# Four-bank score tiles and denominators summed on GpSimd in a graph attention layer

## The chip, the cores and the metric

The kernel runs on one core of a Trainium2 chip. The metric is the device time of one execution in microseconds, lower is better. A core has five engines that run their own instruction queues in order and wait for each other through semaphores: TensorE (PE in the profile, with its weight loads as PEld), VectorE (DVE), ScalarE (ACT), GpSimd (POOL) and SyncE (SP). Matrix products land in PSUM, which has eight banks of 512 fp32 values on each of 128 partitions.

## The reference

Four graph layers are applied to 16 graphs of 1024 nodes with 128 features, each with its own 1024x1024 adjacency of zeros and ones. Each layer normalises the features, takes a relu, computes its own aggregation and adds the result to `x`. The change lies in the second layer, a four-head softmax attention whose scores are offset by the logarithm of the adjacency:

```
def _L1_gnn_ref(x, edge_weight, Wq, bq, Wk, bk, Wv, bv, Wo, bo):
    NH = 4; HD = HID // NH; SCALE = HD ** (-0.5); EPS = 1e-08
    ...
    scores = jnp.einsum('chqd,chkd->chqk', q, k) * SCALE
    scores = scores + jnp.log(jnp.maximum(edge_weight, EPS))[:, None, :, :]
    attn = jax.nn.softmax(scores, axis=-1)
    out = jnp.einsum('chqk,chkd->chqd', attn, v)
    ...
    return out @ Wo.T + bo
```

The third layer (a graph attention without query-key products, `gat` below) and the fourth (a normalised graph convolution, `gcn` below) use the same adjacency and run next to the attention.

## The kernel before

The kernel has three stages, one after another: a dilation of the adjacency, the first layer, and a stage with the other three layers (`attentions_plain`). Only the last one is touched. It starts near 2960 us of the profiled span and lasts to the end.

**Jobs side by side.** The stage loops over the batch `b` from -1 to 16. In each turn `side_by_side` interleaves up to four generators, one step of each at a time by weights: `attend` for graph b (weight 21), `gat` then `gcn` for graph b-1 (45), and `matrix` and `before`, which load the adjacency and make queries, keys and values for graph b+1 (9 each). The order in which the generators emit instructions is only a start: the tile framework then places the instructions in each engine's queue, and puts a semaphore wait on every use of a buffer whose last user is on another engine. A tile of a pool with `bufs=n` can be written again when the use of the n-th tile before it has ended.

**The attention of one graph.** `attend` goes over two halves of 512 query nodes (`hf`), and in each over eight blocks of 128 key nodes (`k`). For one k:

- L1214: four matmuls, one for each head, of 32 rows by 128 columns, give the scores of 128 keys by 512 queries into four PSUM tiles of one bank each (pool `f_ps`, four buffers). They use four different row groups of the array.
- L1217: four matmuls of the adjacency block with 16 times the identity add the logarithm term to each tile.
- L1219: four ACT instructions take the exponential, one bank each, into SBUF tiles `e`.
- L1206 (`weigh`, for the block k-1): four matmuls with the values (`va`) add to one bank `acc`, each head in its own 32 partitions, and four with a matrix of ones (`ones_hd`) add the denominators to a second bank, `den`.

After the eight blocks L1227 takes the reciprocal of the denominators on DVE and L1228 multiplies. An fp32 matmul shows as two records in the trace, so eight records of L1214 are the four heads.

**What runs beside it.** In `gat`, GpSimd multiplies the values by exponentials (L1259, L1261), ACT and DVE split them into three bf16 parts (L677 to L680, a helper), L1289 multiplies A by the parts, and for each head DVE makes a masked matrix `pm` from `dst`, `minus` and A in eight instructions (L1273, function `positive`), which 128 matmuls of L1302 use; DVE reduces each pair of their results (L1304). Two PSUM buffers `sum` serve all of these. L1310 to L1320 close the layer. Each layer's `normal` (L1128 to L1149) is a chain of DVE statistics, a power on GpSimd (L1142) and eight ACT instructions (L1148). `gcn` uses L1326, the splitter, L1338, L1343 and L1350. `matrix` checks each adjacency block on DVE (L1111) and takes a power on GpSimd (L1126). `before` adds a bias on GpSimd (L1178).

Of the kernel before, what the change touches and what calls it, by code (L numbers as in the profile page):

```python
# [7 lines left out]
F32 = mybir.dt.float32  # L8
# [4 lines left out]
AF = mybir.ActivationFunctionType  # L13
ALU = mybir.AluOpType
AX = mybir.AxisListType
PSUM = bass.MemoryType.PSUM
# [3 lines left out]
P = 128  # L20
NB = N // P
H, HD = 4, 32
HN = N // 2
# [986 lines left out]
SIGMA = LOG_EPS / 16.0  # L1010
# [4 lines left out]
def attentions_plain(tc, x1, adj, deg, trouble, eye, Wq, bq, Wk, bk, Wv, bv, Wo, bo, W2, a2, W3, b3, out, bound, reach):  # L1015
    nc = tc.nc
    with ExitStack() as ctx:
        cp = ctx.enter_context(tc.tile_pool(name="f_const", bufs=1))
        small = ctx.enter_context(tc.tile_pool(name="f_small", bufs=4))
        pss = ctx.enter_context(tc.tile_pool(name="f_ps", bufs=4, space=PSUM))  # L1020
        psa = ctx.enter_context(tc.tile_pool(name="f_acc", bufs=2, space=PSUM))
        psg = ctx.enter_context(tc.tile_pool(name="f_sum", bufs=2, space=PSUM))
        xp = ctx.enter_context(tc.tile_pool(name="f_x", bufs=3))
        adp = ctx.enter_context(tc.tile_pool(name="f_adj", bufs=3))
        lp = ctx.enter_context(tc.tile_pool(name="f_load", bufs=2))
        ep = ctx.enter_context(tc.tile_pool(name="f_exp", bufs=8))
        pmp = ctx.enter_context(tc.tile_pool(name="f_pos", bufs=2))
        w2 = ctx.enter_context(tc.tile_pool(name="f_work2", bufs=2))
        w1 = ctx.enter_context(tc.tile_pool(name="f_work1", bufs=1))
# [8 lines left out]
        ident_log = cp.tile([P, P], BF16, name="ident_log")  # L1038
# [3 lines left out]
        ones = cp.tile([P, HD], F32, name="ones_hd")  # L1042
        nc.vector.memset(ones, 1.0)

        def bank(pool=psg, name="sum"):
            return pool.tile([P, HN], F32, name=name)
# [31 lines left out]
        ps = bank()  # L1078
# [13 lines left out]
        ps = bank()  # L1092
# [67 lines left out]
        def natural_times(xT, w, done):  # L1160

            for hf in range(2):
                ps = bank()
                for c in range(4):
                    k = 4 * hf + c
                    nc.tensor.matmul(ps[:, c * P:(c + 1) * P], xT[:, k * P:(k + 1) * P], w, start=True, stop=True)  # L1166
                done(slice(4 * hf, 4 * hf + 4), blocked(ps))
                yield
# [27 lines left out]
        def attend(A, xt, qT, kT, va):  # L1196
            oT = w1.tile([P, N], F32, name="oT")
            for hf in range(2):
                cols = slice(hf * HN, (hf + 1) * HN)
                acc, den = [bank(psa, "acc") for _ in range(2)]  # L1200

                def weigh(k, es):
                    for ps, one in ((acc, False), (den, True)):
                        for hd in range(H):
                            r = slice(hd * HD, (hd + 1) * HD)
                            nc.tensor.matmul(ps[r], ones if one else va[:, k, r], es[hd],  # L1206
                                             start=k == 0, stop=k == NB - 1)

                last = None
                for k in range(NB):  # L1210
                    s = [bank(pss, "t") for _ in range(H)]
                    for hd in range(H):
                        r = slice(hd * HD, (hd + 1) * HD)
                        nc.tensor.matmul(s[hd], kT[r, k * P:(k + 1) * P], qT[r, cols], start=True, stop=False)  # L1214
                    es = []
                    for hd in range(H):
                        nc.tensor.matmul(s[hd], ident_log, A[:, k, cols], start=False, stop=True)  # L1217
                        e = ep.tile([P, HN], F32, name="e")
                        nc.scalar.activation(e, s[hd], AF.Exp, scale=SIGMA)  # L1219
                        es.append(e)  # L1220
                    if last is not None:
                        weigh(k - 1, last)
                    last = es
                    yield
                weigh(NB - 1, last)
                rden = w1.tile([P, HN], F32, name="rden")
                nc.vector.reciprocal(rden, den)  # L1227
                nc.vector.tensor_tensor(oT[:, cols], acc, rden, op=ALU.mult)  # L1228
                yield
            yield from natural_times(oT, wo, lambda c, ps: nc.vector.tensor_tensor(  # L1230
                xt[:, c, :], xt[:, c, :], ps, op=ALU.add))
# [122 lines left out]
        A, ready = {}, {}  # L1354
        for b in range(-1, B + 1):
            jobs = []
            if 0 <= b < B:
                jobs.append((21, attend(A[b], *ready[b])))
            if b >= 1:
                xt = ready[b - 1][0]  # L1360
                jobs.append((45, chain(gat(b - 1, xt, A[b - 1]), gcn(b - 1, xt, A[b - 1]))))
            if b + 1 < B:
                jobs.append((9, matrix(b + 1, A)))
                jobs.append((9, before(b + 1, ready)))
            side_by_side(jobs)
# [49 lines left out]
def whole(tc, x, adj, nodemask, chunk_mats, chunk_mask, eye, sel, p, out):  # L1415
    nc = tc.nc
    with tc.tile_pool(name="dram", bufs=1, space=DRAM) as dp, tc.tile_pool(name="keep", bufs=1) as kp:
        removed = dp.tile([NB, P, P, P], F16, name="removed")
        dilated = dp.tile([B, 2, P, NB, HN], F32, name="dilated")
        x1 = dp.tile([B, N, D], F32, name="x1")  # L1420
        kept = dp.tile([B, P, NB, N], F8, name="kept")
        unsettled = kp.tile([P, 2, NB], F32, name="unsettled")
        trouble = kp.tile([P, B, NB, 3], F32, name="trouble")
        deg = kp.tile([P, B, NB], F32, name="degree")
        bound = kp.tile([P, B], F32, name="bound")
        reach = kp.tile([P, B], F32, name="reach")
        word = kp.tile([1, 1], I32, name="word")
        g = lambda *names: [p["L0_gnn_" + n] for n in names]
        layer0 = [g("Wr1", "Wr2", "Wr3"), g("Wx1", "Wx2", "Wx3"), g("b1", "b2", "b3"), g("g1", "g2", "g3"),
                  g("be1", "be2", "be3"), *g("Wl", "bl")]  # L1430
        weights = [p["L1_gnn_" + n] for n in ("Wq", "bq", "Wk", "bk", "Wv", "bv", "Wo", "bo")]
        weights += [p["L2_gnn_W"], p["L2_gnn_a"], p["L3_gnn_W"], p["L3_gnn_b"]]
        dilate_plain(tc, adj, eye, kept, unsettled)
        convolutions_plain(tc, x, eye, kept, x1, *layer0)
        attentions_plain(tc, x1, adj, deg, trouble, eye, *weights, out, bound, reach)
        verdict(tc, nodemask, unsettled, trouble, deg, bound, reach, word)
        with tc.If(nc.values_load(word[0:1, 0:1], min_val=0, max_val=6 * P) > 0):
            dilate(tc, adj, nodemask, chunk_mats, chunk_mask, removed)
            convolutions(tc, x, adj, nodemask, eye, removed, dilated, x1, *layer0)
            attentions(tc, x1, adj, eye, sel, *weights, out)  # L1440
# [40 lines left out]
```

## Time and profile before

| | |
|---|---|
| median of 3 runs | 5915.55 us (5912.04 to 5918.76) |
| profiled execution, its time | 5929.54 us |
| profiled execution, its span | 5927.7 us |
| PE busy | 4577.2 us, 77% |
| DVE busy | 2813.5 us, 47% |
| ACT busy | 1999.0 us, 34% |
| POOL busy | 1086.7 us, 18% |
| in 2940 to 5760 us: PE, DVE, ACT, POOL busy | 2455.90, 1555.66, 1166.30, 345.81 us |
| granted TensorE clock in 2940 to 5760 us | 0.93 |

The steady turns of the stage (graphs 1 to 15) can be told apart by the first L1289 of each. Two of these starts, 4010.88 and 4194.56 us, are 183.7 us apart, and over all fifteen turns the mean is 180.9 us. In the profile, busy time counts an engine's instructions, a line "idle before" names what ended the wait, and the granted clock is the share of full TensorE speed that was allowed. A POOL or DVE instruction that is held up after it has started shows as a longer instruction, not as a wait.

### The profile page before, as it was taken

The numbers are of one execution on the slowest core, as the hardware profiler recorded it, in microseconds if no ns is written. First come the engines' busy times: TensorE is split into PE (matmuls) and PEld (weight loads), VectorE is DVE, ScalarE is ACT, GpSimd is POOL, SyncE is SP. The second block draws the span as 40 slices with busy tenths as digits, with TensorE's granted clock in tenths as the row PEclk, the third lists the DMA queues.
The fourth block names the chain that finished last, engine by engine and source line by source line (L and its number), as shares of the span: only waits on it lengthen the run. The fifth ranks groups of instructions, "written<-read, shape, count | busy, mean of one in ns | idle before, by whom it ended". The sixth has DMA issues, their size and how long they took to land. (4 is left out here: it accounts for less than half of the span.)

```text
span 5927.7 us, 71034 instructions
## 1 busy us (share of the span) xinstructions
PE 4577.2 (77%) x29914; PEld 2489.5 (42%) x29914; DVE 2813.5 (47%) x4098; ACT 1999.0 (34%) x3265; POOL 1086.7 (18%) x719
## 2 busy tenths in 40 slices
PE   5777775666658886776498888888888888888884
PEld 3444442434344454444334344344343343434443
DVE  4555443222253234323445565555655555555455
ACT  3444443122122221222264344443344434344321
POOL 5611111111140005103511011110111101111001
PEclk8898987777779987998799999999899999999997
DMA  8600004111002211220511011110011100110000
GB/s 277 179 1 1 1 4 161 44 36 43 29 22 71 79 64 43 75 75 15 154 60 33 4 36 36 36 36 11 26 36 36 36 22 15 36 36 29 4 2 8
DMA packets 260322, 283.41 MB, mean 48 GB/s; under 512 B 10508, under 2 KB 225176, under 8 KB 251800
## 3 DMA queue, kind: packets, MB, share of 16 engines
q1 hardware_dynamic: 110232, 203.27, 10.1%
q10 hardware_dynamic: 149760, 75.51, 4.4%
q8 instruction: 236, 3.87, 0.3%
q14 instruction: 94, 0.77, 0.0%
HBM read 228.40 MB, written 50.33 MB: 47 GB/s over the span
## 5 line engine op out<-in xcount | busy, mean ns | idle before, releaser
L1214 PE MATMUL t<-qT,kT 32*128 32x512 f32 x2048 | 550.7, 700 | 205.7 <-ACT e L1219 205.4
L963 PE MATMUL t<-C,parts 128*128 128x512 fp8e4 x2304 | 593.4, 416 | 129.6 <-DVE parts L680 88.3
L1219 ACT ACTIVATE e<-t 128x512 f32<-128x512 f32 x1024 | 530.6, 601 | 471.3 <-PE t L1217 471.1
L1273 DVE SCALAR_TENSOR_TENSOR pm<-dst,minus,A 128x1024 fp8e4<-128x1024 f32 x512 | 646.9, 1334 | 89.8 <-ACT dst L1270 89.8
L1302 PE MATMUL sum<-parts,pm 128*128 128x198 bf16 x4096 | 400.2, 254 | 103.3 <-DVE pos L1304 103.3
L1302 PEld LDWEIGHTS <-pm 128*128 128x128 fp8e4 x4096 | 357.0, 99 | 260.2 <-issue 254.1
L963 PEld LDWEIGHTS <-parts 128*128 128x128 bf16 x2304 | 237.8, 105 | 449.9 <-DVE parts L680 110.6
L968 DVE TENSOR_TENSOR o<-t,rdeg 128x1024 f32<-128x1024 f32 x48 | 58.7, 1224 | 667.4 <-PE t L238 667.4
L1214 PEld LDWEIGHTS t<-qT,kT 32*128 32x128 f32 x2048 | 189.3, 198 | 360.6 <-ACT e L1219 263.2
L219 POOL TENSOR_TENSOR nrm<-nrm,minus_half 128x8 f32<-128x8 f32 x48 | 104.1, 2169 | 1272.7 <-DVE nrm L976 1272.7
L1206 PE MATMUL acc<-e,va 128*32 128x512 f32 x2048 | 329.8, 659 | 0.0
L1206 PE MATMUL acc<-e,ones_hd 128*32 128x512 f32 x2048 | 327.9, 625 | 0.0
L846 PE MATMUL big<-tri,rows 128*128 128x256 fp8e4 (+3 forms) x1344 | 319.3, 375 | 0.0
L1217 PE MATMUL t<-A,ident_log 128*128 128x512 fp8e4 x1024 | 299.8, 415 | 0.0
L1311 POOL TENSOR_TENSOR pos<-pos,ex 128x1056 f32<-128x1056 f32 x16 | 49.0, 3063 | 1306.5 <-DVE pos L1304 1306.5
L225 PE MATMUL t<-ident,h 128*128 128x128 f32 x512 | 88.4, 322 | 252.9 <-ACT h L255 147.1
L851 DVE SCALAR_TENSOR_TENSOR rows<-y,hh,rows 128x1024 fp8e4<-128x1024 f16 x128 | 185.4, 1448 | 196.5 <-ACT y L849 195.3
L1227 DVE RECIPROCAL rden<-acc 128x512 f32<-128x512 f32 x32 | 107.4, 3358 | 355.1 <-PE acc L1206 355.1
L1304 DVE TENSOR_REDUCE pos<-sum 128x132 f32<-128x396 f32 x256 | 141.0, 566 | 271.0 <-PE sum L1302 271.0
L861 ACT CAST rows<-big 128x1024 fp8e4<-128x1024 f32 x128 | 129.5, 1012 | 376.7 <-PE big L860 304.9
L965 ACT COPY aggT<-t 128x1024 f32<-128x1024 f32 x48 | 48.6, 1012 | 562.0 <-PE t L963 562.0
L1270 ACT COPY dst<-sum 128x512 f32<-128x512 f32 x128 | 75.1, 588 | 458.3 <-PE sum L1269 458.3
(256 smaller groups left out, 7989.9 us busy)
## 6 DMA issues: line engine op xcount, KB each, us to landing
a<-in_adj_dram SPq DMA_DIRECT2D x128, 512.0 KB, 3.8
C<-kept SPq DMA_DIRECT2D x48, 1024.0 KB, 4.7
x<-xt ACTq DMA_DIRECT2D x48, 512.0 KB, 2.9
kept<-rows SPq DMA_DIRECT2D x16, 1024.0 KB, 3.8
xt<-in_x_dram ACTq DMA_DIRECT2D x32, 512.0 KB, 3.8
xt<-x ACTq DMA_DIRECT2D x32, 512.0 KB, 3.8
a_row<-in_adj_dram SPq DMA_DIRECT2D x16, 512.0 KB, 6.1
x<-x ACTq DMA_DIRECT2D x16, 512.0 KB, 4.0
```

The lines of the kernel that those rows point to most:

```text
L846: nc.tensor.matmul(ps[:, a:lo + HN], lhs, triF[:, a - t * P:lo + HN - t * P], start=t == 0, stop=t == NB - 1 or t == 3 and lo == 0)
L851: nc.vector.scalar_tensor_tensor(row, y16, hh[:, g:g + 1], row, op0=ALU.not_equal, op1=ALU.mult, saturate=False)
L861: nc.scalar.copy(m[:, g, :, s * P:(s + 1) * P], tr, saturate=False)
L963: nc.tensor.matmul(ps[:, cols], parts[:, k, j, :], C[:, j, cols], start=j == 0 and k == 0, stop=j == NB - 1 and k == 2)
L1206: nc.tensor.matmul(ps[r], ones if one else va[:, k, r], es[hd], start=k == 0, stop=k == NB - 1)
L1214: nc.tensor.matmul(s[hd], kT[r, k * P:(k + 1) * P], qT[r, cols], start=True, stop=False)
L1217: nc.tensor.matmul(s[hd], ident_log, A[:, k, cols], start=False, stop=True)
L1219: nc.scalar.activation(e, s[hd], AF.Exp, scale=SIGMA)
L1227: nc.vector.reciprocal(rden, den)
L1273: nc.vector.scalar_tensor_tensor(pm[:, i, :], dst, minus[:, i, hd:hd + 1], A[:, i, :], op0=ALU.is_ge, op1=ALU.mult, saturate=False)
L1302: nc.tensor.matmul(ps[:, jj * 6 * W:(jj + 1) * 6 * W], pm[:, i, (j + jj) * P:(j + jj + 1) * P], flat(parts4[:, i, hd]), start=i == 0, stop ...
L1304: nc.vector.reduce_sum(pos[:, j:j + 2, hd, :], ps[:, :12 * W].rearrange("p (j s w) -> p j w s", j=2, s=3), axis=AX.X)
```

## The change

The four score tiles of one bank each become one tile of four banks, allocated from a pool with one buffer. The four exponential tiles become one tile of 128x2048 (three buffers), and ACT takes two heads, 1024 elements, in one instruction: 512 instructions in place of 1024. The ones matmuls inside the loop go; instead GpSimd adds each block's exponentials into `total` (128x2048 fp32, seven adds for each half of a graph, 224 in all), and after the last block four matmuls of ones with `total` give the denominators. `weigh(NB - 1)` is followed by one more `yield`.

```
-        pss = ctx.enter_context(tc.tile_pool(name="f_ps", bufs=4, space=PSUM))
+        pss = ctx.enter_context(tc.tile_pool(name="f_ps", bufs=1, space=PSUM))
...
-        ep = ctx.enter_context(tc.tile_pool(name="f_exp", bufs=8))
+        ep = ctx.enter_context(tc.tile_pool(name="f_exp", bufs=3))
...
                 acc, den = [bank(psa, "acc") for _ in range(2)]
 
-                def weigh(k, es):
-                    for ps, one in ((acc, False), (den, True)):
-                        for hd in range(H):
-                            r = slice(hd * HD, (hd + 1) * HD)
-                            nc.tensor.matmul(ps[r], ones if one else va[:, k, r], es[hd],
-                                             start=k == 0, stop=k == NB - 1)
+                total = w1.tile([P, H, HN], F32, name="total")
+
+                def weigh(k, es, before):
+                    for hd in range(H):
+                        r = slice(hd * HD, (hd + 1) * HD)
+                        nc.tensor.matmul(acc[r], va[:, k, r], es[:, hd], start=k == 0, stop=k == NB - 1)
+                    if k:
+                        nc.gpsimd.tensor_tensor(total, before if k == 1 else total, es, op=ALU.add)
 
                 last = None
                 for k in range(NB):
-                    s = [bank(pss, "t") for _ in range(H)]
+
+                    s = pss.tile([P, H, HN], F32, name="t")
                     for hd in range(H):
                         r = slice(hd * HD, (hd + 1) * HD)
-                        nc.tensor.matmul(s[hd], kT[r, k * P:(k + 1) * P], qT[r, cols], start=True, stop=False)
-                    es = []
+                        nc.tensor.matmul(s[:, hd], kT[r, k * P:(k + 1) * P], qT[r, cols], start=True, stop=False)
+                    es = ep.tile([P, H, HN], F32, name="e")
                     for hd in range(H):
-                        nc.tensor.matmul(s[hd], ident_log, A[:, k, cols], start=False, stop=True)
-                        e = ep.tile([P, HN], F32, name="e")
-                        nc.scalar.activation(e, s[hd], AF.Exp, scale=SIGMA)
-                        es.append(e)
+                        nc.tensor.matmul(s[:, hd], ident_log, A[:, k, cols], start=False, stop=True)
+                        if hd % 2:
+                            nc.scalar.activation(es[:, hd - 1:hd + 1], s[:, hd - 1:hd + 1], AF.Exp, scale=SIGMA)
                     if last is not None:
-                        weigh(k - 1, last)
+                        weigh(k - 1, last, first)
                     last = es
+                    first = es if k == 0 else first
                     yield
-                weigh(NB - 1, last)
+                weigh(NB - 1, last, first)
+                yield
+                for hd in range(H):
+                    nc.tensor.matmul(den[hd * HD:(hd + 1) * HD], ones, total[:, hd], start=True, stop=True)
                 rden = w1.tile([P, HN], F32, name="rden")
                 nc.vector.reciprocal(rden, den)
                 nc.vector.tensor_tensor(oT[:, cols], acc, rden, op=ALU.mult)
```

## The prediction

> **What bounds the kernel now.** I read the page's groups first, then the waits of the last stage, then the timeline of one steady turn of the batch loop. The page says what the attention costs PE and what stands beside it on ACT and DVE:
>
> ```profile
> span 5927.7 us, 71034 instructions
> ...
> L1214 PE MATMUL t<-qT,kT 32*128 32x512 f32 x2048 | 550.7, 700 | 205.7 <-ACT e L1219 205.4
> L1219 ACT ACTIVATE e<-t 128x512 f32<-128x512 f32 x1024 | 530.6, 601 | 471.3 <-PE t L1217 471.1
> L1273 DVE SCALAR_TENSOR_TENSOR pm<-dst,minus,A 128x1024 fp8e4<-128x1024 f32 x512 | 646.9, 1334 | 89.8 <-ACT dst L1270 89.8
> ```
>
> PE is the busiest engine (2455.90 of 2820 us between 2940 and 5760), so at first sight its work sets the time. The view of PE's waits in the stage shows the rest, each line with its total, count and longest:
>
> ```profile
> PE t L1214 <- ACT e L1219: 205.4, 61, 6.9
> PE sum L1302 <- DVE pos L1304: 103.3, 34, 8.1
> PE sum L1289 <- DVE parts L680: 46.8, 14, 18.8
> ```
>
> So two places have no slack: where PE waits for DVE, anything that slows DVE is paid at once. The timeline shows them in a turn:
>
> ```profile
> 4179.97 2.82 POOL L1178 TENSOR_TENSOR x<-x,bor 128x1024 f32<-128x1024 f32 x1 [3.76 <-issue]
> 4180.51 11.74 DVE L1273 SCALAR_TENSOR_TENSOR pm<-dst,minus,A 128x1024 fp8e4<-128x1024 f32 x8
> 4192.17 2.34 DVE L680 TENSOR_TENSOR parts<-vals,parts 128x2112 bf16<-128x2112 f32 x1
> ...
> 4194.56 11.44 PE L1289 MATMUL sum<-parts,A 128*128 128x396 bf16 x64 [1.86 <-DVE parts L680]
> ```
>
> Eight pm instructions, then parts, then PE may begin L1289. For each later head it is the same:
>
> ```profile
> 4022.16 1.95 PE L1269 MATMUL sum<-hT,wdst 128*128 128x512 f32 x4
> 4024.76 9.66 DVE L1273 SCALAR_TENSOR_TENSOR pm<-dst,minus,A 128x1024 fp8e4<-128x1024 f32 x8 [1.84 <-ACT dst L1270]
> 4034.34 1.04 DVE L1304 TENSOR_REDUCE pos<-sum 128x132 f32<-128x396 f32 x2
> 4034.95 0.22 PE L1118 MATMUL sum<-A,ident 128*128 128x128 fp8e4 x1 [2.28 <-DVE pos L1304]
> ```
>
> The third thing to see is what a GpSimd instruction does to such a DVE instruction:
>
> ```profile
> 4110.51 2.34 POOL L1326 TENSOR_TENSOR x<-x,b3r 128x1024 f32<-128x1024 f32 x1 [5.62 <-ACT h L1148]
> 4110.97 3.03 DVE L678 TENSOR_TENSOR h<-h,gparts 128x512 f32<-128x512 f32 x2 [5.68 <-ACT gparts L677]
> ...
> L1312 DVE TENSOR_TENSOR tot<-tot,ex 128x1056 f32<-128x1056 f32 x16 | 46.9, 2930 | 0.6
> L1314 DVE TENSOR_TENSOR tot<-tot,pos 128x1056 f32<-128x1056 f32 x16 | 20.1, 1258 | 1.7
> ```
>
> L1312 and L1314 have one shape, but L1312 runs while POOL runs L1311 and takes 1.67 us longer. A lone L678 takes 0.69 us; here the first ends only after POOL has ended at 4112.85. L1273 goes from a minimum of 1270 to a maximum of 3374 ns (the view of its line), and the group at 4180.51 is 2.1 us longer than that at 4024.76, with L1178 beside it. DVE instructions with two SBUF inputs and GpSimd's tensor_tensor take turns, whole instruction by whole instruction; L1178, at 2.82 against 2.34, shows that GpSimd waits its turn too.
>
> **What the Trainium skill says.** "GPSIMD Engine Reference", Specifications, says that GpSimd shares SBUF interfaces with VectorE, with contention for instructions that have two SBUF inputs; the lines above agree and give the size. Its section with measured numbers gives 4497 ns for an fp32 add of 2048 elements. "TensorE: Matmul & The Clock Gate", Part 3, says that column tiles run concurrently and a pack lasts about one matmul; Part 1 there says that an idle window of about 3.4 us halves the clock. The trace agrees with both: 16 records of L1206 occupy 1.86 us, one matmul alone (two records, 4031.62) still 1.05, and after a 5.99 us wait L1214 takes 3.52 in place of 1.14. "PSUM — Partial Sum Buffer", PSUM bank collisions, asks for separation by bank only; the waits of the four-bank tile below therefore come from tracking the tile, not from a need.
>
> **The change part by part.** I counted the instruction order of the two built kernels.
>
> PE work: eight matmuls of `weigh` as one run cost 1.86, so without other effects 256 x 0.93 = 238 go and 32 x 0.97 = 31 come back: -207. But the order no longer keeps them together. Before, the L1206 runs need 556 rounds of up to four; after, the values need 390 (204 are pairs) and the denominators 60. At 0.93 and 0.97 that is 517 against 436: -81. Score runs fall from 393 to 375, -19 at 1.06. Identity matmuls stand mostly in pairs, about 0.53 each against 0.95 for four: +24. The net is -76 us, 5 a turn.
>
> Waits: in the new order the third identity matmul of a block waits for the first exponential of the same block, and the first score matmul for the second one of the block before. An exponential of 1024 I take at 1.03 (a 128x1024 ACT copy from PSUM, L965, is 1012 ns; bounds 0.98 to 1.2). With 0.19 from PE to ACT and 0.04 back, it costs 1.26; a pair of value matmuls hides 0.97. Where the side jobs put L1302 or L1338 there, nothing is seen. Going through one turn I find five gaps of 0.3, one of 1.26 and some of 0.1: 3.3 us a turn. ACT gets less work, and that is worth nothing, since its delays are those of DVE and POOL results ahead in its queue.
>
> GpSimd: an add of 2048 costs from 3.9 (twice L1259's 1.96) to 5.9 (L1311's 3.06 for 1056, scaled). I take 4.6, twice the L1326 row's 2.34 less a fixed part; 14 a turn are 64 us on an engine with some 20 us of work. The sum fits, the turns with DVE do not. I walked the new order through a turn, with the durations above, from its first identity matmul (before: 4151.29, or 3967.6 one turn earlier):
>
> L1289: pm(0) starts on DVE at +29, as before (4180.51). The adds for k=2 and k=3 become ready at 29.6 and 35.5, both inside pm(0), and take 9.2; L1178 now runs ahead, which gives back 2.1. The next add stands behind L1126, which waits for DVE. So 29 + 9.7 + 9.2 + 2.3 = 50 against 43.3: +7. PE would have been ready at 38.
>
> pm(1): the add for k=4 ends 1.4 into it, that for k=5 falls inside it (4.6). +6 and some 2 of extra PE blocks: the next L1269 stands at 87 against 72, +15.
>
> pm(2): the add for k=6 overlaps 1.5, that for k=7 4.6; the denominator matmuls wait for this last add, 2.5 us, inside the same delay. Next L1269 113.6 against 92.4: +21.
>
> pm(3): no add falls in it, since the first block of a half has none.
>
> End of gat: add k=10 gets between L1312 and L1314, +5, and the normalisation behind it holds ACT and so the next exponentials. With PE blocks done meanwhile, L1338 starts at 173 against 155: +18. The tail, three blocks with `gcn` and the second denominators in place of one, adds 6. A turn is 24 us longer; the PE saving and the round trips are in it.
>
> Clock: the waits of 12 and 10 us at L1289 and pm(1), and 13 at the normalisation, make about three more cold starts; each costs some 2 us (3.52 less 1.14). I take 5 a turn, bounds 0 and 8.
>
> Turn 0 has no gat; its blocks take 5 us now and about as much with adds of 4.6; +5 for two exposed last adds.
>
> 15 x (24 + 5) + 5 = 440 on 5929.54 gives 6370 for an execution like the profiled one. The median of runs lies 14 us lower, so 6355.
>
> **The rivals.** First, the collisions are mostly hidden: waits on PE move but DVE catches up. Then -76 + 16 x 3.3 + 16 x 2.5 leaves +17: 5930, up to 6080 with some collisions. The 47% of DVE busy time speaks for it, the zero slack at L680 and pos against it.
>
> Second, faster: the PE saving decides, since PE is the busiest engine. With the -76 alone 5840; with all fours concurrent, 5710. It decides if the adds cost the path less than one add (5 us) a turn. Against it stand the two adds inside pm(0).
>
> Third, heavier: nearly every add lands on the path, or lasts 5.5 and more. 14 x 4.6 less 5 is 59 a turn, 6800.
>
> That the four-bank tile doesn't give four banks of look-ahead is already in the forecast: pairs wait for each other.
>
> **How the numbers follow.** Forecast 0.63, hidden 0.16, faster 0.07, heavier 0.14. Its own bounds (add 3.9 to 5.9, clock 0 to 8, three or seven colliding adds) give 6150 to 6550; reaching a little to both sides, 6110 to 6590. A measurement of this kernel can't tell less than about 0.2% from none. Faster 0.08, same 0.02, slower 0.90.
>
> **What would show it.** Right: L1279 (the pm line after the change) with a mean of 1.7 us or more, POOL L1209 near 4.6 us, PE's wait for parts grown from 46.8 to 150 us or more and that for pos from 103 to 200 or more, and a turn of about 210 us between first L1295s (the new number of L1289). Value pairs at about 0.97 each show the lost saving. Wrong: pm unchanged beside adds, or a turn under 185 us.

## The result and the profile after

The changed kernel takes 6412.28 us (median of 4 runs, 6403.48 to 6419.01). The kernel before took 5917.16 us beside it (4 runs, 5912.04 to 5948.53), so the ratio is 1.0824, with a 95% interval of 1.0784 to 1.0864. The profiled span grew from 5927.7 to 6417.3 us, by 489.6.

The page of the changed kernel has these lines, in the columns known from before:

```profile
span 6417.3 us, 66960 instructions
...
L1209 POOL TENSOR_TENSOR total<-total,e 128x2048 f32<-128x2048 f32 x192 | 898.2, 4678 | 818.4 <-ACT e L1222 817.8
L1279 DVE SCALAR_TENSOR_TENSOR pm<-dst,minus,A 128x1024 fp8e4<-128x1024 f32 x512 | 906.1, 1838 | 90.6 <-ACT dst L1276 90.6
L1222 ACT ACTIVATE e<-t 128x1024 f32<-128x1024 f32 x512 | 522.8, 1021 | 1141.0 <-PE t L1220 1136.9
...
L1209 POOL TENSOR_TENSOR total<-e 128x2048 f32<-128x2048 f32 x32 | 146.0, 4561 | 540.1 <-ACT e L1222 538.5
```

L1279 is the old L1273, unchanged in the code. Its instruction grew from 1334 to 1838 ns, 512 times. PE's waits over the span are:

```profile
PE t L1220 <- ACT e L1222: 325.5, 110, 13.8
PE sum L1295 <- DVE parts L680: 187.5, 16, 18.4
PE sum L1118 <- DVE pos L1310: 116.8, 14, 8.3
PE sum L1308 <- DVE pos L1310: 110.3, 34, 8.3
```

The wait for parts was 46.8. That for pos, at the matmuls of `positive` and at L1118, the identity matmul behind them, was 103.3 and 32.8, 136.1 in all; it is now 110.3 and 116.8, 227.1 in all, so the growth stands at L1118. Its line before was:

```profile
PE sum L1118 <- DVE pos L1304: 32.8, 14, 3.1
```

The timeline of a steady turn shows the first of these waits arise:

```profile
4187.85 18.16 DVE L1279 SCALAR_TENSOR_TENSOR pm<-dst,minus,A 128x1024 fp8e4<-128x1024 f32 x8
4188.62 4.87 POOL L1209 TENSOR_TENSOR total<-total,e 128x2048 f32<-128x2048 f32 x1 [2.91 <-ACT e L1222]
4195.16 4.98 POOL L1209 TENSOR_TENSOR total<-total,e 128x2048 f32<-128x2048 f32 x1 [1.67 <-ACT e L1222]
4205.94 2.35 DVE L680 TENSOR_TENSOR parts<-vals,parts 128x2112 bf16<-128x2112 f32 x1
4208.33 5.12 PE L1295 MATMUL sum<-parts,A 128*128 128x396 bf16 x16 [10.60 <-DVE parts L680]
```

The eight pm instructions took 11.74 us before. Two additions of 4.87 and 4.98 fall inside them, and the eight take 18.16. PE stands for 10.60 us. The second head meets the same:

```profile
4220.73 4.51 POOL L1209 TENSOR_TENSOR total<-total,e 128x2048 f32<-128x2048 f32 x1 [9.73 <-ACT e L1222]
...
4224.79 14.14 DVE L1279 SCALAR_TENSOR_TENSOR pm<-dst,minus,A 128x1024 fp8e4<-128x1024 f32 x8 [1.84 <-ACT dst L1276]
4230.07 5.38 POOL L1209 TENSOR_TENSOR total<-total,e 128x2048 f32<-128x2048 f32 x1 [4.83 <-ACT e L1222]
4239.46 0.26 PE L1118 MATMUL sum<-A,ident 128*128 128x128 fp8e4 x1 [8.34 <-DVE pos L1310]
```

Where the 489.6 us lie is read from the first L1295 of each turn (L1289 before) and the first score matmul of the stage:

| part of the span | before | after | difference |
|---|---|---|---|
| up to the first score matmul | 2961.7 | 2970.7 | 9.0 |
| from there to the first L1295 (turn 0) | 134.6 | 179.1 | 44.5 |
| fifteen turns, mean of one | 180.86 | 209.86 | 15 x 29.0 = 435.0 |
| last first-L1295 to the end | 118.4 | 119.7 | 1.3 |

The first row cannot be put down to the change: over all kernels below, which differ only in code behind it, that start scatters between 2954.1 and 2978.6 us.

### The profile page after: what moved, and what is told of

Same layout as the page of the kernel before. It is cut to its first block, busy times and chain, and to the rows that moved or that the text cites. A ratio compares the mean times of both kernels' runs of the same rounds, so it can differ in the third digit from the quotient of the medians.

```text
span 6417.3 us, 66960 instructions
## 1 busy us (share of the span) xinstructions
PE 4612.0 (72%) x28122; PEld 2425.8 (38%) x28122; DVE 3170.0 (49%) x4098; ACT 1986.5 (31%) x2753; POOL 2117.9 (33%) x943
## 4 chain that ended last, share of the span: by engine, by line
PE 46%; DVE 30%; ACT 9%; POOL 8%; issue 4%; DMA 3%; SPq 0%; ACTq 0%; POOLq 0%; DVEq 0%
DVE pm L1279 14%; PE t L963 8%; PE sum L1308 4%; PE t L238 4%; PE big L846 3%; PE sum L1295 3%; PE sum L1344 3%; PE acc L1207 3%; DVE rows L851 3%; PE t L1217 2%; PE t L1220 2%; PE stat L981 2%; DVE h L678 2%; PE stat L991 1%; DVE h L930 1%
## 5 line engine op out<-in xcount | busy, mean ns | idle before, releaser
L1209 POOL TENSOR_TENSOR total<-total,e 128x2048 f32<-128x2048 f32 x192 | 898.2, 4678 | 818.4 <-ACT e L1222 817.8
L1279 DVE SCALAR_TENSOR_TENSOR pm<-dst,minus,A 128x1024 fp8e4<-128x1024 f32 x512 | 906.1, 1838 | 90.6 <-ACT dst L1276 90.6
L1222 ACT ACTIVATE e<-t 128x1024 f32<-128x1024 f32 x512 | 522.8, 1021 | 1141.0 <-PE t L1220 1136.9
L963 PE MATMUL t<-C,parts 128*128 128x512 fp8e4 x2304 | 592.6, 416 | 130.8 <-DVE parts L680 89.7
L1308 PE MATMUL sum<-parts,pm 128*128 128x198 bf16 x4096 | 433.3, 265 | 110.3 <-DVE pos L1310 110.3
L1207 PE MATMUL acc<-e,va 128*32 128x512 f32 x2048 | 490.3, 688 | 0.3
L1217 PE MATMUL t<-qT,kT 32*128 32x512 f32 x2048 | 474.4, 717 | 12.5 <-ACT e L1222 7.5
L1111 DVE SCALAR_TENSOR_TENSOR junk<-a 128x1024 fp8e4<-128x1024 f32 x128 | 177.7, 1388 | 415.4 <-DMA a<-in_adj_dram 414.8
L1295 PE MATMUL sum<-parts,A 128*128 128x396 bf16 x1024 | 221.9, 380 | 187.5 <-DVE parts L680 187.5
L1209 POOL TENSOR_TENSOR total<-e 128x2048 f32<-128x2048 f32 x32 | 146.0, 4561 | 540.1 <-ACT e L1222 538.5
L1220 PEld LDWEIGHTS <-ident_log 128*128 128x128 bf16 x1024 | 82.8, 101 | 598.2 <-issue 583.0
L853 POOL TENSOR_TENSOR own<-rows,lower 128x256 bf16<-128x256 fp8e4 x128 | 99.1, 774 | 627.9 <-DVE rows L851 316.1
```

The lines of the kernel that those rows point to most:

```text
L963: nc.tensor.matmul(ps[:, cols], parts[:, k, j, :], C[:, j, cols], start=j == 0 and k == 0, stop=j == NB - 1 and k == 2)
L1207: nc.tensor.matmul(acc[r], va[:, k, r], es[:, hd], start=k == 0, stop=k == NB - 1)
L1209: nc.gpsimd.tensor_tensor(total, before if k == 1 else total, es, op=ALU.add)
L1217: nc.tensor.matmul(s[:, hd], kT[r, k * P:(k + 1) * P], qT[r, cols], start=True, stop=False)
L1220: nc.tensor.matmul(s[:, hd], ident_log, A[:, k, cols], start=False, stop=True)
L1222: nc.scalar.activation(es[:, hd - 1:hd + 1], s[:, hd - 1:hd + 1], AF.Exp, scale=SIGMA)
```

## The experiments

Each kernel ran beside the kernel before. All at one view, by the kind of score tile and by where the denominators come from, with the ratio to the kernel before and its interval:

| | ones matmuls in the loop | added on GpSimd | added on VectorE | no additions |
|---|---|---|---|---|
| four tiles of one bank | (before) 1 | 1.0805 [1.0787, 1.0823] | 0.9999 [0.9989, 1.0008] | not run |
| one tile of four banks | 1.0237 [1.022, 1.0254] | (after) 1.0824 [1.0784, 1.0864] | 1.0033 [1.0025, 1.0041] | 1.009 [1.0073, 1.0107] |
| two tiles of two banks | 1.0081 [1.0061, 1.0101] | not run | 1.0059 [1.0043, 1.0075] | not run |

The theory was that of the forecast: a GpSimd addition and a VectorE instruction with two SBUF inputs exclude each other for whole instructions, so that the additions stop the pm instructions (called masked rows in some expectations). The rival was that the four-bank tile, with its single buffer, holds the scores back.

**No additions.** From the changed kernel the GpSimd instruction is taken out, and the final ones matmuls read the last block's exponentials.

```
-                    if k:
-                        nc.gpsimd.tensor_tensor(total, before if k == 1 else total, es, op=ALU.add)
...
-                    nc.tensor.matmul(den[hd * HD:(hd + 1) * HD], ones, total[:, hd], start=True, stop=True)
+                    nc.tensor.matmul(den[hd * HD:(hd + 1) * HD], ones, last[:, hd], start=True, stop=True)
```

> The changed kernel without GpSimd's 224 adds; the four matmuls of ones take the exponentials of the last node block alone, so the sums over the other seven blocks are left out of the denominators. Tiles, exponentials and waits stay as in the changed kernel. Exclusion theory (GpSimd's adds and DVE's instructions with two SBUF inputs take turns): nearly everything comes back, 5850 to 6000 us, L1273's successor (pm) at a mean of 1.30 us, PE's wait for parts below 60 us. Look-ahead theory (one four-bank tile makes PE and ACT wait for each other): about 6350 us, since only the adds go. A result near 6150 would make both half right.

Measured: 5975.57 us. The page shows pm back at its undisturbed duration:

```profile
span 5979.2 us, 66451 instructions
...
L1276 DVE SCALAR_TENSOR_TENSOR pm<-dst,minus,A 128x1024 fp8e4<-128x1024 f32 x512 | 619.2, 1281 | 94.6 <-ACT dst L1273 94.6
```

PE's wait for parts is 57.0 us. So 437 of the 495 us of the medians are the additions; 52 to 58 are the net of the rest: the tile, the wider exponential, and the ones matmuls, which are fewer and stand at the end. Not all of the 437 us is exclusion: in the changed kernel PE also waits for the total itself, 45.4 us in 17 waits.

**The tile alone.** The four-bank tile and the exponential of two heads, with the ones matmuls in the loop as before.

```
+                    for ps, one in ((acc, False), (den, True)):
+                        for hd in range(H):
+                            r = slice(hd * HD, (hd + 1) * HD)
+                            nc.tensor.matmul(ps[r], ones if one else va[:, k, r], es[:, hd],
+                                             start=k == 0, stop=k == NB - 1)
```

> Only the first half of the change: four-bank tiles and exponentials of two heads, but the denominators by ones matmuls inside the loop as before, no GpSimd. In the order of the built kernel the value and ones matmuls need 724 rounds of up to four in place of 556, at 0.95 us that is 160 us more of PE. Exclusion theory: 5930 plus that and some 40 of round trips, about 6050 to 6130 us, with pm at 1.30 us. Look-ahead theory: 6300 us or more.

Measured: 6061.23 us, 138 more than the 5923.02 us of the kernel before in this comparison. The loss looks like a wait for the single tile, but PE's waits for exponentials are smaller than before (124.3 and 62.4 us against 205.4). PE's work grew instead, from 4577.2 to 4757.1 us. The groups of PE between 2900 and 6100 us show where, first before, then with the tile alone:

```profile
L1206 PE MATMUL acc<-e,va 128*32 128x512 f32 x2048 | 329.8, 659 | 0.0
L1206 PE MATMUL acc<-e,ones_hd 128*32 128x512 f32 x2048 | 327.9, 625 | 0.0
```

```profile
L1207 PE MATMUL acc<-e,ones_hd 128*32 128x512 f32 x2048 | 582.4, 637 | 0.0
L1207 PE MATMUL acc<-e,va 128*32 128x512 f32 x2048 | 467.1, 640 | 0.1
```

The counts agree and the means nearly, the time they occupy does not: records that ran beside each other no longer do. In PE's order before, 210 of the 312 unbroken runs of value and ones matmuls hold all eight of a block; with the tile alone the most frequent runs hold five and three. In rounds of up to four matmuls that is 724 against 556. At the forecast's 0.93 us a round this is an estimate of 156 us, near the 180 by which PE's busy time grew. (The two lines overlap, so their sum says too much: together they occupy 846.3 us against 582.3, and the score matmuls 458.7 against 550.7.)

These two kernels split the loss. The tile and its wider exponential cost 138 us. Taking the ones matmuls out of the loop gives 86 of them back (6061.23 to 5975.57, with PE's busy time down from 4757.1 to 4539.6). GpSimd's additions then cost 437. The sum is 489.

**The additions alone.** Four tiles of one bank and single exponentials as before, with GpSimd's additions and the ones matmuls at the end.

```
-                        nc.scalar.activation(e, s[hd], AF.Exp, scale=SIGMA)
-                        es.append(e)
+                        nc.scalar.activation(es[:, hd], s[hd], AF.Exp, scale=SIGMA)
...
+                    if k:
+                        nc.gpsimd.tensor_tensor(total, before if k == 1 else total, es, op=ALU.add)
```

> Only the second half of the change: one-bank score tiles with four buffers and exponentials one head at a time as before, but GpSimd adds them up and four ones matmuls close each half. The value and ones matmuls need 345 rounds in place of 556, so PE has 200 us less to do. Exclusion theory: the DVE path sets the turns all the same, 6200 to 6380 us, pm at 1.75 us or more. Look-ahead theory: below the kernel before, 5750 to 5850 us.

Measured: 6395.23 us, 15 above the expected range and far from the rival's. The net cost is 472 us without any four-bank tile, so the rival falls; pm takes 2106 ns. In this kernel and in the changed one 90 of the 224 additions overlap a pm instruction, but for 410 us in all here and for 340 there. PE's waits lie elsewhere in this order, too: 27.2 us for parts, but 198.2 at L1166 behind ACT's L1123.

**Filled waits.** Forty identity matmuls, whose result nobody reads, are put ahead of L1295 in the changed kernel, to keep PE at work while it waits for parts.

```
+            ps = bank()
+            for n in range(5 * NB):
+                nc.tensor.matmul(ps, ident16, A[:, n % NB, 0:HN], start=True, stop=True)
```

> The changed kernel with 40 matmuls of 128x512 more in each turn, whose results nobody reads, put before the first product of A and parts, where PE waits 10 to 11 us for DVE. They keep PE busy there and change nothing else. If the halved clock after that wait costs what the trace shows, L1295's 64 matmuls take 11.4 us in place of 13.9 and the time falls by 15 x 2.5, to about 6375 us. If the clock is most of the loss, it falls by 100 us or more. If DVE is late again behind it, nothing changes: 6400 to 6420 us.

Measured: 6459.64 us, 47 more than the changed kernel. The expectation failed. The timeline shows the filling and the stretch behind it, of which only the first matmuls are shown:

```profile
4198.21 18.20 DVE L1279 SCALAR_TENSOR_TENSOR pm<-dst,minus,A 128x1024 fp8e4<-128x1024 f32 x8
...
4204.69 7.07 PE L1293 MATMUL sum<-A,ident 128*128 128x512 fp8e4 x32
...
4218.74 11.06 PE L1298 MATMUL sum<-parts,A 128*128 128x396 bf16 x48 [6.98 <-DVE parts L680]
```

The fillers end at 4211.8, and PE still stands for 6.98 us. The view of windows (its bounds, its length, then PE, PEld, DVE, ACT and POOL busy with their counts, the granted clock, and DMA) shows full speed under the fillers and a low clock right behind them:

```profile
4204.00:4212.00 8.00, 7.75 (x36) 3.43 (x35) 8.00 (x4) 1.02 (x1) 4.50 (x1) 1.00 0.05 19
4212.00:4218.70 6.70, 0.00 (x0) 0.00 (x0) 6.70 (x7) 0.00 (x0) 0.00 (x0) 0.63 0.00 0
4218.70:4236.00 17.30, 17.26 (x85) 7.90 (x85) 6.63 (x13) 2.05 (x2) 4.05 (x2) 0.85 0.00 0
```

The clock's records put the half clock at 4213.8 to 4224.0 here and at 4202.7 to 4213.0 in the changed kernel: in both some 15 us after pm begins, so that about 5 us of the stretch, which begins 20.5 us after pm, run at half clock (a granted share of 0.5). The wait that remained did not keep the clock up. The fillers also moved a group of scores into the stretch, whose 64 records now take 16.8 us from first to last in the median, against 14.1. What the slower clock costs this kernel was not measured by this run.

**Half the additions.** GpSimd adds heads 0 and 1 alone.

```
-                        nc.gpsimd.tensor_tensor(total, before if k == 1 else total, es, op=ALU.add)
+                        nc.gpsimd.tensor_tensor(total[:, 0:2], before[:, 0:2] if k == 1 else total[:, 0:2], es[:, 0:2],
+                                                op=ALU.add)
```

> The changed kernel, but GpSimd adds up heads 0 and 1 alone: 1024 elements an add in place of 2048. The denominators of heads 2 and 3 come from the last node block alone, so their sum over the blocks is left out. The number of adds, their places in the queue, the score tile, the exponentials and TensorE's matmuls stay. Theory of the exclusion (VectorE's two-input operations stand still for as long as a GpSimd add runs, so the price goes with GpSimd's busy time): an add falls from 4.68 us to about 2.35 us, and the 437 us between the changed kernel (6412) and the one without any adds (5976) fall to about half: 6150 to 6240 us; the mean masked row near 1560 ns, between 1281 and 1838. Rival (the price is the wait for a total or for a buffer of exponentials, or an instruction's fixed cost): 6350 to 6430.

Measured: 6130.35 us, ratio 1.0354 [1.0332, 1.0376], pm 1533 ns. That is 20 us under the expected range: half the length costs 155 of 437 us, or 35%. The price goes with the length of the additions, but more steeply than in proportion. Of the additions, 192 of the 224 take 2772 ns in the mean against some 2340 where nothing is beside them, so GpSimd also waits for VectorE. One place shows the exclusion at its plainest, on an instruction of 8 elements that otherwise takes 167 ns:

```profile
4267.29 1.64 POOL L1142 TENSOR_TENSOR ln_st<-ln_st,minus_half 128x8 f32<-128x8 f32 x1 [3.68 <-DVE ln_st L1140]
4268.89 2.35 POOL L1209 TENSOR_TENSOR total<-e 128x1024 f32<-128x1024 f32 x1
4268.96 2.30 DVE L1146 SCALAR_TENSOR_TENSOR ln_st<-ln_st 128x8 f32<-128x8 f32 x1 [1.75 <-POOL ln_st L1142]
4271.29 0.49 ACT L1148 ACTIVATE h_a<-x,ln_st 128x128 f32<-128x128 f32 x1 [1.24 <-DVE ln_st L1146]
```

L1146 starts 0.07 us after the addition, ends with it, and the normalisation on ACT comes 2.1 us late.

**The additions on VectorE.** One word is changed in the changed kernel.

```
-                        nc.gpsimd.tensor_tensor(total, before if k == 1 else total, es, op=ALU.add)
+                        nc.vector.tensor_tensor(total, before if k == 1 else total, es, op=ALU.add)
```

> The changed kernel with the 224 additions on VectorE in place of GpSimd, nothing else. No run has shown a 128x2048 add there; the add of 128x2112 took 2.36 us on VectorE, so some 2.3 us, half of GpSimd's 4.68. Theory of the exclusion: on GpSimd each add takes its whole 4.68 us from VectorE when VectorE has two-input work, so moving it there halves the price: 437 us to about 220, in all 6150 to 6260 us, masked rows back near 1280 ns. Rival (GpSimd works beside VectorE and the price is that the total is late): VectorE gets 224 x 2.3 = 515 us of new work in its queue, ahead of parts and masked rows, and the time is 6450 to 6650 us.

Measured: 5938.52 us, better than either theory expected. VectorE took 457 us more of busy time than in the kernel before, and the time rose by 0.33%. Its page:

```profile
L1279 DVE SCALAR_TENSOR_TENSOR pm<-dst,minus,A 128x1024 fp8e4<-128x1024 f32 x512 | 641.6, 1324 | 111.1 <-ACT dst L1276 111.1
...
L1209 DVE TENSOR_TENSOR total<-total,e 128x2048 f32<-128x2048 f32 x192 | 438.5, 2284 | 205.5 <-ACT e L1222 205.2
```

The same additions at the same places in the program cost 474 us less on the engine that is busier. What cost the time was not VectorE's load, but GpSimd holding VectorE up. The error of the expectation, as the lines below suggest, was to charge VectorE's 2.28 us to the path as if no idle time were near. In the turn's first part the additions stand behind the eight pm instructions, not between them, and one of them runs while PE is already at L1295:

```profile
4185.14 11.36 DVE L1279 SCALAR_TENSOR_TENSOR pm<-dst,minus,A 128x1024 fp8e4<-128x1024 f32 x8 [1.69 <-ACT dst L1276]
...
4198.70 2.28 DVE L1209 TENSOR_TENSOR total<-total,e 128x2048 f32<-128x2048 f32 x1
...
4204.31 2.27 DVE L1209 TENSOR_TENSOR total<-total,e 128x2048 f32<-128x2048 f32 x1
4204.44 2.92 PE L1295 MATMUL sum<-parts,A 128*128 128x396 bf16 x9 [1.23 <-DVE parts L680]
```

Why this kernel is 37 us faster than the one without additions is not settled; another order on PE and 491 against 709 us at half clock, from the first score matmul to the end, go with it.

**Two tiles of two banks.** The denominators by ones matmuls in the loop, exponentials of two heads.

```
-                    s = pss.tile([P, H, HN], F32, name="t")
+                    s = [pss.tile([P, 2, HN], F32, name="t") for _ in range(2)]
...
+                            nc.scalar.activation(es[hd // 2], s[hd // 2], AF.Exp, scale=SIGMA)
```

> The kernel before (denominators by matmul with ones in the loop) with two score tiles of two banks in place of four of one bank, and exponentials of two heads each; four buffers of two heads. Theory of the single tile: the 138 us that the four-bank tile alone cost (6061 against 5923) come from the one buffer, whose next scores wait for the second exponential of the block before; with two tiles that wait is as short as with four, and 5860 to 5960 us follows, ScalarE having about 1030 ns for two heads in place of two of 600. Rival (the loss is the wider exponential's, or TensorE's order around it): 6000 to 6070.

Measured: 5962.37 us, 2 over the expected range. Two tiles win back 99 of the 138 us, yet not by a shorter wait: PE waits 209.1 us at its score matmuls for exponentials, as long as before. PE's busy time is back at 4575.6, and the value and ones matmuls stand in 543 rounds (724 with one tile, 556 before). Their lines in the same window:

```profile
L1207 PE MATMUL acc<-e,va 128*32 128x512 f32 x2048 | 315.7, 658 | 0.0
L1207 PE MATMUL acc<-e,ones_hd 128*32 128x512 f32 x2048 | 308.1, 614 | 0.0
```

So the split runs above are what the two tiles mended: the expectation's number was nearly met, but its reason, a shorter wait, was wrong. The remaining 0.8% was not traced.

**Two tiles and additions on VectorE.** 448 additions of 1024 elements, six buffers of two heads.

```
-                        nc.gpsimd.tensor_tensor(total, before if k == 1 else total, es, op=ALU.add)
+                        for i in range(2):
+                            nc.vector.tensor_tensor(totals[i], before[i] if k == 1 else totals[i], es[i], op=ALU.add)
```

> The denominators added up as in the changed kernel, but on VectorE and by two heads (448 additions of 1024 elements, about 1.2 us each, for 224 of 2048 at 2.28), with two score tiles of two banks in place of the one of four, and six buffers of two heads. Theory (the two prices are separate: the GpSimd additions, and the single score tile that the next scores wait for): the tile's price falls by what two tiles gave with matmul denominators (5962 for 6061, 99 us), TensorE keeps the saving of the ones matmuls that the additions on VectorE showed, and the time is at or below the kernel before: 5840 to 5925 us. Rival (VectorE, with some 550 us of new work in the stage, now sets the turns; the tile no longer matters): 5930 to 6010.

Measured: 5959.77 us, the rival's number: the two gains do not add up. A new wait stands in PE's list, which the kernel before does not show among its largest:

```profile
PE t L1219 <- ACT e L1224: 125.6, 70, 7.0
PE sum L1346 <- ACT gparts L677: 122.5, 16, 17.6
```

L1346 is `gcn`'s product. Its input follows the normalisation, a chain of small VectorE instructions, and that chain now reaches ACT later than PE is ready. In the turn near 4100 us, four of the additions (at 4131.73, 4134.00, 4136.68 and 4138.05 us, 1.2 us each) stand between instructions of this chain and just ahead of it. So VectorE's queue has become the limit at that place.

**A copy in place of the addition.** GpSimd copies the block with one input and adds nothing.

```
-                        nc.gpsimd.tensor_tensor(total, before if k == 1 else total, es, op=ALU.add)
+                        nc.gpsimd.tensor_copy(total, es)
```

> The changed kernel with each of the 224 additions turned into a GpSimd copy of the same 2048 numbers with one input: the sum over the node blocks is left out, and the denominators come from the last copied block. The places, tiles and waits stay. How long such a copy takes no run has shown; from nothing saved (4.7 us) to half (2.3). Theory that any GpSimd instruction on these buffers stops VectorE's two-input work: the price goes with the copies' busy time as it did with the adds' (437 us for 1048 us busy, 155 for 500 to 600): 6130 us at 2.3 us a copy, to 6410 at 4.7, masked rows 1550 to 1840 ns. Rival that only two-input GpSimd instructions do: masked rows near 1285 ns and 5960 to 6030 us whatever the copies take.

Measured: 6085.91 us, ratio 1.0274 [1.0252, 1.0295]. The page:

```profile
L1209 POOL COPY total<-e 128x2048 f32<-128x2048 f32 x224 | 458.7, 2048 | 1556.6 <-ACT e L1222 1555.0
L1279 DVE SCALAR_TENSOR_TENSOR pm<-dst,minus,A 128x1024 fp8e4<-128x1024 f32 x512 | 717.5, 1472 | 90.1 <-ACT dst L1276 90.1
```

With 459 us of copies pm takes 1472 ns and the time is 110 us over the kernel without additions. So a GpSimd instruction with one input holds VectorE up as well; the rival's 1285 ns and 6030 us fall. The time is 44 us under the 6130 expected for a copy of 2.3 us. In part the copy is shorter, 2.05; an estimate from the half additions (155 us for 609 us of them) gives 117 us for 459 us of copies, near the 110 measured.

**One-bank tiles and additions on VectorE.** The kernel before with nothing of the change but the added denominators, on VectorE.

```
+                    if k:
+                        nc.vector.tensor_tensor(total, before if k == 1 else total, es, op=ALU.add)
```

> The kernel before with its four score tiles of one bank and exponentials of one head each, and of the change only the denominators added up over the node blocks, on VectorE (224 additions of 2048 elements, 2.28 us each) in place of GpSimd; three buffers of four heads. Theory of two separate prices: without the four-bank tile (52 us without additions) and without the GpSimd additions nothing of the change's loss is left, and the saving of the ones matmuls on TensorE shows: 5860 to 5925 us, at or below the kernel before. Rival (VectorE's queue now holds up the value pairs and the masked rows, as it did with the two score tiles, where 5960 came out): 5930 to 6000.

Measured: 5925.77 us against 5927.32 for the kernel before in these runs: no difference that can be told, at the edge between the two expectations. TensorE did not get the saving that the theory gave it: PE is busy for 4615.1 us against 4577.2. The score matmuls stand in 450 runs against 393 and occupy 671.5 us against 550.7:

```profile
L1217 PE MATMUL t<-qT,kT 32*128 32x512 f32 x2048 | 671.5, 713 | 119.3 <-ACT e L1221 118.4
```

A part of PE's busy time is also the clock (614 us of the stage at half clock against 443), and the wait for `gcn`'s input is here too, 103.6 us. So taking the ones matmuls out of the loop was worth 86 to 123 us where the one four-bank tile stood (6061.23 to 5975.57 without additions, to 5938.52 with VectorE's), and brought no clear net gain with tiles of one or two banks. One-bank tiles without any additions were not run, so how the saving and VectorE's additions offset each other there stays open. No version run here beats the kernel before.

## Why the prediction was right

The direction, the main mechanism and nearly the size were right: 6355 forecast, 6412 measured, inside 6110 to 6590. Of its signs, pm (1838 ns), POOL L1209, the wait for parts (187.5) and the turn (209.9) came as written. The wait for pos did so only with L1118; at the matmuls of `positive` themselves it went from 103.3 to 110.3. By its own steps:

- **GpSimd's additions.** The addition was taken at 4.6 us and measures 4678 and 4561 ns. The walk through one turn can be laid beside the timeline from 4159.31, where the turn's first identity matmul stands. L1295 was put at +50 and starts at +49.0 (4208.33). The next L1275, for head 2, was put at +87 and starts at +89.7 (4249.00), that for head 3 at +113.6 and starts at +117.3. The first L1344 was put at +173 and starts at +177.2, and the turn ends at +211.6, where the walk, which leaves the clock out, has 207.7. Two additions fell inside pm(0), one and the end of another inside pm(1) and inside pm(2), none inside pm(3), and one lies over L1320, which went from 1258 to 5128 ns in the mean, as forecast:

```profile
L1320 DVE TENSOR_TENSOR tot<-tot,pos 128x1056 f32<-128x1056 f32 x16 | 82.0, 5128 | 1.7
```

The kernels without additions, with half additions, with copies and with additions on VectorE show that this is the cause.
- **A turn.** +29 was forecast (24 and 5 for the clock), +29.0 measured. This exactness is partly luck: without the additions the forecast's own steps give a turn 1.7 us shorter (5 of PE work saved, 3.3 of round trips), but the kernel without additions has turns of 182.94 us, 2.1 longer. The additions and the clock then cost 26.9 a turn, not the 30.7 implied. Two errors of 3.8 us cancel.
- **PE work and the round trips.** The net of these two had the wrong sign: -76 and +53 were forecast, and without additions the kernel is 52 us slower than before. The parts were taken from the wrong place. The round trips were to show as PE's waits for exponentials; without additions these are 213.7 us against 205.4. (In the changed kernel they are 333.0, so most of that growth goes with the additions.) The tile's price lies in PE's order instead: 138 us alone, of which the ones matmuls give 86 back. And PE's work is not time one for one: between these two kernels its busy time falls by 217.5 us and the time by 86, while its wait at L1156 for normalised features, for one, grows from 8.0 to 37.1. Against the kernel before PE is busy 38 us less without additions and 43 less with VectorE's, though both are slower. Where the rest of the 52 us lies was not traced.
- **The clock.** From the first score matmul to the end the records show 1139 us at half clock against 443 before, so the direction was right. The price of a cold start was misread: in the 3.52 us of L1214 at 4183.27 the four heads begin 0.48 us apart, each behind an exponential of the block before. A halved clock explains some 1.14 of the 2.38 us (an estimate: the usual 1.14 doubled); the rest goes with these exponentials. The 64 records of L1295 take 14.08 us in the median against 11.44, of which the 16 shown above at 5.12 us, beside 32 in 5.80, are the reason. The 5 us a turn as a whole could not be isolated, because the filled waits did not keep the clock up; the 3.9 us by which the turn's end lies behind the walk is near it, but its cause was not separated.
- **Turn 0: the mis-sized term.** "+5 for two exposed last adds" measured +44.5. The step supposed that a block takes about as long as an addition, so that only the last one shows. The chain of waits, followed back through this turn (start, length, what), shows that the additions themselves are the chain:

```profile
3032.21 5.56 POOL total L1209
3037.84 4.53 POOL total L1209
3042.43 4.51 POOL total L1209
3046.98 1.94 PE acc L1231 x8
...
3079.62 4.53 POOL total L1209
3084.22 4.53 POOL total L1209
3088.82 4.51 POOL total L1209
3093.37 1.94 PE acc L1231 x8
```

The last three of the first half and all seven of the second follow each other with gaps under 0.1 us up to the ones matmuls (L1231). Beside the little other work of this turn, an addition lasts longer than the block it belongs to, and the denominators wait for the last. Turn 0 takes 146.3 us without additions, 150.1 with VectorE's and 179.1 with GpSimd's, against 134.6 before: some 12 us of the 44.5 are the tile's and the end's, 33 the additions on GpSimd. The walk was made for the steady turn and not for this one; that and the uncertain 9 us at the stage's start are what 6370 for the profiled execution lacked to the measured one.

**The rivals.** "Hidden" falls with pm at 1838 ns; 5930, its time, is what came out when the additions stood on VectorE (5938.52). "Faster" falls: the two additions inside pm(0) were not hidden, and even without any additions the tile's price is larger than what the ones matmuls give back. "Heavier" falls: 437 us for 224 additions is 1.95 us an addition, not the whole 4.6.

## What to carry to other kernels

Work for GpSimd that reads and writes SBUF, as the additions and copies here, can be paid in VectorE's time too: before moving it there, find in the timeline which two-input VectorE instructions it will lie beside, and whether one of them has a waiting engine behind it. The same work on the busier VectorE can cost less: here it took half the time there, and it ran between the instructions that matter and did not stretch them. Count what a change of tile does to the order of the matmuls that run beside each other: here that order, and not the wait for the tile, was the price of the wider tile. Walk the fill turn of a pipeline separately from the steady turn, since side jobs that cover a chain in one can be missing in the other.

## What the runs showed of the hardware beyond that

- The exclusion does not reach every VectorE instruction. In the changed kernel's timeline a reduction from PSUM starts 0.03 us after an addition and takes its usual time, as does the reduction of one SBUF input at L1192 (1219 ns with an addition over 14 of its 16 instances, 1212 for its twin, which met none):

```profile
4249.17 4.51 POOL L1209 TENSOR_TENSOR total<-total,e 128x2048 f32<-128x2048 f32 x1 [13.72 <-ACT e L1222]
4249.20 0.57 DVE L1310 TENSOR_REDUCE pos<-sum 128x132 f32<-128x396 f32 x1 [4.00 <-PE sum L1308]
```

- Sorted by whether an addition overlaps them, the changed kernel's 371 pm instructions without overlap take 1279 ns in the mean and the 141 with overlap 3310, at most 5551.
- A GpSimd copy of 128x2048 fp32 holds VectorE's pm instructions up like an addition (2093 ns in the mean for the 120 that meet one, 1283 for the others); it takes 2048 ns, the addition 4678, and the addition on VectorE 2284.
- In a PE wait of 6.98 us, right behind 7.07 us of unbroken filling at full clock, a stretch of 10.2 us at half clock began, as long as the one that began in the unfilled wait of 10.60 us.
